# A four-layer graph network on one core: own-feature work of 12 tiles moved to the start of layer 1, and another way to end layer 2

## The chip, the core and the metric

The kernel runs on one core of a Trainium2 chip. The metric is the device time in microseconds of one execution, the median of several runs. TensorE is PE (its weight loads PEld), VectorE is DVE, ScalarE is ACT, GpSimd is POOL, SyncE is SP. DMAs are issued from the queues of SP, ACT and POOL; the indirect ones, that gather rows by an index column, from POOL.

## The reference

A graph of 6250 nodes (49 tiles of 128) and 100,000 edges, sorted by destination (782 tiles of 128 edges). The destinations crowd at low nodes, so that tile 0 alone takes over 14,000 edges.

```python
h = relu(layernorm(x))                                    # 256 features
h = h @ W1_self + mean(h[src] by dst) @ W1_neigh + b1     # layer 1, 512
hp = relu(h @ W2_pool + b2_pool)
h = h @ W2_self + max(hp[src] by dst) @ W2_neigh + b2     # layer 2
h = ((sum(h[src] by dst) + h) / (deg + 1)) @ W3_neigh + b3
h = h @ W4_self + mean(h[src] by dst) @ W4_neigh + b4
out = x + h @ W_fc + b_fc
```

The kernel multiplies weights together beforehand, so that a layer's result is not formed where only its products are needed. Layer 1 writes hp (with Wa = W1_self W2_pool and Wb = W1_neigh W2_pool), layer 2 writes r.

## The kernel before, in words

`fast_path` has a prologue and four layers.

**Layer 1** (`sums`, L442, with `done1`, L1094) makes sums over neighbours in two ways. The edges of node tiles 0 to 7 go through count matrices: `build` makes one-hot tiles (ACT L337 and L338, DVE L340), PE counts with them (L346), and `dense` multiplies the counts with the node rows Z1 that stay on the chip (L564). These pieces are a list that `Hub` steps through, paced by the gathers. The edges from tile 308 on, for node tiles 8 to 48, are gathered: for each of 474 edge tiles POOL gathers 128 rows of `tab_h` into a ring of 14 (L483), DVE makes a one-hot of the destinations (L479), PE multiplies three bf16 parts into `pg` (L505), and after each group of four DVE adds `pg` to the accumulators of the node tiles that the group can hold (L534). A planner (`g_of`) gives each node tile a first and a last group; tile 37's last is 173 of 195, tile 48's is 195. When the last one is in, `done1(d)` is queued: a generator of which one step is taken for each gather, two at a time in flight. It forms the mean m1 (ACT L1103), turns the node's own features h0 (six products of Z1 with a bf16 identity, L1111) and m1 (two f32 transposes, L1114) into one PSUM bank, copies all of it to `th` (ACT L1116), stores `th` in `tab_t` (SP L1117, 256 KB), multiplies the own half with Wa (L1124) and the other half with Wb (L1127) into one bank, adds the bias row `crow` (DVE L1130), applies Relu (ACT L1131) and stores hp in `tab_p` (SP L1132). A list `aside` has work of which one step is taken for each gather too: `tail_checks` (20 steps on DVE) and `segments` (68 steps, with twelve loads on SP).

**Layer 2** walks the edges in another order: six blocks of 52, 100, 220, 180, 130 and 100 steps, the last block first. A step gathers 128 rows of hp (POOL L1475, 256 KB), and DVE keeps a running maximum along each partition's stretch of edges (L1456). Every second row tile is stored in `rows2` (SP L1460). A node's edges can run on from one partition to the next. So at a block's end `carry(b, last)` turns the last row tile (L1316), makes a scan along the partitions (L1324, L1328), gathers the rows where the partitions' first nodes end (POOL L1331, index `fixI`), turns the carry back (L1339), takes the maximum with it (DVE L1342) and stores the result in a part of `rows2` of its own (SP L1343). Then a node tile is begun by `done2(d)`: `totals` gathers its maximum from each block that can hold its edges (POOL L1351; four buffers) and loads `th` back (ACT's queue L1357); `done2` takes the maximum over blocks (DVE L1366), transposes (L1370, ACT L1373), multiplies `th` with usA (L1377) and usB (L1380), the maximum with un (L1383), and splits the result into three bf16 parts (L1391 to L1399), stored as r in `tab_r` (L1400). Tiles are begun last one first, none while a block's carry is under way, at least 11 steps apart and no faster than `NT * (at - FIRST_AT) / (T - 20 - FIRST_AT)`, FIRST_AT being 112. Tiles 6 to 37 are also used at once for layer 3's products (`early_products`, L564 with `ae`; their sums are added at L1241), 1/32 of what is left for each step. By the planner only tile 0 has edges in block 0, the last one that is worked; it also has some in block 1. Tile 1 has edges in blocks 1 and 2, tiles 2 to 9 in block 2 alone. `node_rows` (`finding`) works out the rows that the totals are gathered from, some steps at a time.

**Layers 3 and 4** gather r and its product again with `sums`; layer 3 can gather only when all of `tab_r` is written.

Instructions of one engine run in the order in which the framework lays them out. That order follows the program, but an instruction can stand earlier than where the program has it; `keep_in_program_order` forbids that for one instruction.

Of the kernel before, what the change touches and what calls it, by code (L numbers as in the profile page):

```python
# [9 lines left out]
F32 = mybir.dt.float32  # L10
BF16 = mybir.dt.bfloat16
# [4 lines left out]
ALU = mybir.AluOpType  # L16
# [4 lines left out]
P = 128  # L21
# [11 lines left out]
FIRST_AT = 112  # L33
# [44 lines left out]
def fast_path(  # L78
# [15 lines left out]
    nc = tc.nc  # L94
    N, FI = x.shape
    E = src.shape[0]
    FH = W1_self.shape[1]
# [7 lines left out]
    KI = FI // P  # L105
# [978 lines left out]
    with ExitStack() as on:  # L1084
# [6 lines left out]
        def h0_row(s):  # L1091
            return Z1[:, s, :]

        def done1(d, acc):  # L1094
            r = rmean[:, d : d + 1]
            nc.vector.tensor_copy(deg[:, d : d + 1], acc[:, FI : FI + 1])
            nc.vector.tensor_scalar_max(r, acc[:, FI : FI + 1], 1.0)
            nc.vector.reciprocal(r, r)
            o = only[:, d : d + 1]
            nc.vector.tensor_scalar(o, acc[:, FI + 1 : FI + 2], float(P), None, op0=ALU.mult)  # L1100
            nc.vector.tensor_add(o, o, acc[:, FI + 2 : FI + 3])
            m1 = wk.tile([P, FI], F32, name="m1")
            nc.scalar.activation(m1, acc[:, :FI], AF.Copy, scale=r)  # L1103
            yield 1
            yield 1
            yield 1
            pt = bank(pst, "pt", "pt_m", (2 * KI, P))
            for k in range(KI):
                for part in range(3):
                    c = part * FI + k * P  # L1110
                    nc.tensor.matmul(pt[:, k, :], Z1[:, d, c : c + P], ident_b,  # L1111
                                     start=(part == 0), stop=(part == 2))
            for k in range(KI):
                nc.tensor.transpose(pt[:, KI + k, :], m1[:, k * P : (k + 1) * P], ident)  # L1114
            th = wk.tile([P, 2 * KI, P], F32, name="th")
            nc.scalar.copy(th, pt)  # L1116
# [6 lines left out]
            for k in range(KI):  # L1123
                nc.tensor.matmul(ph, th[:, k, :], Wa[:, k, :], start=(k == 0), stop=False)  # L1124
            yield 1
            for k in range(KI):
                nc.tensor.matmul(ph, th[:, KI + k, :], Wb[:, k, :], start=False,  # L1127
                                 stop=(k == KI - 1))
            hp = wk.tile([P, FH], F32, name="hpf")
            nc.vector.tensor_add(hp, ph, crow)  # L1130
# [10 lines left out]
        for d in range(H1):  # L1141
            work += merged(denses[d], builds[d + 1]) if d + 1 < H1 else denses[d]
        hub = Hub(made.rest() + work)
        sums(wk, psg, tab_h, FI, srcT, keyT, JC * P, H1, done1, 14, hub, counts=3, todo=todo, rest=24,
             aside=[tail_checks(wk), segments()])
    layer1.close()


    def node_rows(pool, psm):
# [28 lines left out]
        for b, tb in reversed(list(enumerate(BLOCKS))):  # L1178
# [26 lines left out]
            nc.vector.tensor_scalar(pF, pF, float(kept[b] * P + 1), None, op0=ALU.add)  # L1205
            nc.vector.tensor_sub(pF, pF, t_)
            nc.vector.tensor_mul(pF, pF, off)
            nc.vector.tensor_add(t_, t_, pF)
# [9 lines left out]
        for k in range(4):  # L1218
# [6 lines left out]
                nc.vector.tensor_tensor(over[:, H1:], lim[:, k, H1:], beg[:1, H1:], op=ALU.is_gt)  # L1225
            nc.vector.tensor_reduce(bad[:1, 4 + k : 5 + k], over, AX.X, ALU.max)


    span3 = ctx.enter_context(tc.tile_pool(name="span3", bufs=1))
    jb = g_of[H3][0] * G  # L1230
# [15 lines left out]
    with tc.tile_pool(name="fl2c", bufs=1) as ck, ExitStack() as late:  # L1246
# [66 lines left out]
        def carry(b, last):  # L1313
# [7 lines left out]
            for k in range(KH):  # L1321
# [9 lines left out]
            nc.gpsimd.indirect_dma_start(  # L1331
                out=fix, out_offset=None, in_=rows2[0 : run_at[b] + n_of[b] - P, :],
                in_offset=bass.IndirectOffsetOnAxis(ap=fixI[:, b : b + 1], axis=0),
# [9 lines left out]
            nc.sync.dma_start(runs[b][n_of[b] - P :, :], fix)  # L1343
            for _ in range(4):
                yield

        def totals(d):
            tots = []
# [118 lines left out]
        for b in reversed(range(NB)):  # L1467
# [57 lines left out]
            next(end)  # L1525
            ends.append(end)
            last_b = b
        for _ in finding:
            pass
        for _ in end:  # L1530
            pass
        tiles += [d for d in reversed(range(NT)) if b_of[d][0] == 0]
        while tiles or now:
            if tiles and len(now) < 2:
                now.append(done2(tiles.pop(0)))
            for g in list(now):
                if next(g, 0) == 0:
                    now.remove(g)
# [776 lines left out]
```

## Time and profile before

| what | us |
|---|---|
| median of 3 runs (2750.1 to 2760.69) | 2751.69 |
| profiled execution, its own time | 2753.24 |
| its span | 2751.4 |
| layer 1's gathers, first to last issue | 104.9 to 712.7 |
| layer 2's first gather of X | 738.26 |
| layer 2's last gather of X is issued | 1833.91 |
| layer 3's first gather | 1873.46 |

Times within the profile count from the start of the span. A row of the timeline gives start, duration, engine, line, operation, the tiles written and read, and in brackets how long the engine had been idle and what ended that. A row by stretch gives for each engine the busy time and the number of instructions in it, then the granted clock of PE as a share of the full one, the share of the DMA engines' time that was used, and GB/s. A row of a group gives the count, the busy time and the mean in ns of one record; a product in f32 with 512 columns leaves two records. A DMA that POOL issues is busy only while it is being issued; the data land later.

### The profile page before, as it was taken

The numbers are of one execution on the slowest core, as the hardware profiler recorded it, in microseconds if no ns is written. First come the engines' busy times: TensorE is split into PE (matmuls) and PEld (weight loads), VectorE is DVE, ScalarE is ACT, GpSimd is POOL, SyncE is SP. The second block draws the span as 40 slices with busy tenths as digits, with TensorE's granted clock in tenths as the row PEclk, the third lists the DMA queues.
The fourth block names the chain that finished last, engine by engine and source line by source line (L and its number), as shares of the span: only waits on it lengthen the run. The fifth ranks groups of instructions, "written<-read, shape, count | busy, mean of one in ns | idle before, by whom it ended". The sixth has DMA issues, their size and how long they took to land.

```text
span 2751.4 us, 39155 instructions
## 1 busy us (share of the span) xinstructions
PE 2372.0 (86%) x11540; PEld 1281.9 (47%) x11671; DVE 2071.6 (75%) x5542; ACT 906.2 (33%) x2177; POOL 1942.6 (71%) x2267
## 2 busy tenths in 40 slices
PE   3578999999887666798899969976999999999998
PEld 2245666776553322343344424432444444565554
DVE  8888777765599898789889988862667776466665
ACT  5467777763278786321311111110000101000000
POOL 6477777776467776777777777744777776677775
PEclk9799999999898787899999989998999999999999
DMA  9566777777699999999999999978999998888886
GB/s 286 154 170 192 208 211 217 229 220 211 207 362 356 328 360 340 364 352 350 327 358 356 359 340 340 343 251 313 373 380 389 387 368 303 259 239 241 240 243 198
DMA packets 350747, 806.43 MB, mean 293 GB/s; under 512 B 56014, under 2 KB 147638, under 8 KB 350492
## 3 DMA queue, kind: packets, MB, share of 16 engines
q0 software_dynamic: 146160, 514.05, 56.8%
q1 hardware_dynamic: 137784, 207.04, 20.7%
q10 hardware_dynamic: 66580, 82.73, 9.0%
q8 instruction: 94, 1.54, 0.2%
q14 instruction: 129, 1.06, 0.1%
HBM read 605.25 MB, written 199.17 MB: 292 GB/s over the span
## 4 chain that ended last, share of the span: by engine, by line
PE 32%; DMA 27%; DVE 8%; issue 5%; POOL 3%; ACT 0%; ACTq 0%; SPq 0%; DVEq 0%; POOLq 0%
DMA X<-rows,srcIf 12%; PE pd L564 11%; PE pg L505 6%; PE pd L556 4%; DMA rows<-X 3%; DVE run L1456 3%; DMA ring<-tab_r,srcE 3%; DMA ring<-tab_s,srcE 3%; DVE X L1456 2%; PE pd L557 2%; POOL X L1475 2%; PE pg L500 2%; PE pm_prf L1383 2%; DMA zt<-tab_r 2%; PE pm_prf L1377 1%
## 5 line engine op out<-in xcount | busy, mean ns | idle before, releaser
L1475 POOL DMA_INDIRECT X<-rows,srcIf x782 | 744.1, 952 | 276.4 <-issue 148.2
L1456 DVE SCALAR_TENSOR_TENSOR run<-run,samef,X 128x512 f32<-128x512 f32 x758 | 571.4, 754 | 45.3 <-DMA X<-rows,srcIf 41.4
L505 PE MATMUL pg<-ring,hot 128*128 128x259 bf16 (+1 forms) x2432 | 516.0, 322 | 68.4 <-DMA ring<-tab_h,srcT 39.5
L483 POOL DMA_INDIRECT ring<-tab_h,srcT x474 | 455.6, 961 | 157.6 <-issue 58.5
L534 DVE SCALAR_TENSOR_TENSOR acc<-pg,M,acc 128x256 f32<-128x256 f32 (+2 forms) x694 | 356.8, 539 | 116.0 <-PE pg L505 83.8
L483 POOL DMA_INDIRECT ring<-tab_r,srcE x342 | 333.7, 976 | 132.0 <-issue 59.4
L564 PE MATMUL pd<-r,ae 128*128 128x512 bf16 x1493 | 367.6, 384 | 37.2 <-DVE acc L1241 35.1
L483 POOL DMA_INDIRECT ring<-tab_s,srcE x314 | 299.8, 955 | 116.5 <-PE pg L501 35.2
L505 PEld LDWEIGHTS <-hot 128*128 128x128 bf16 x2448 | 240.3, 99 | 278.7 <-issue 120.1
L1456 DVE SCALAR_TENSOR_TENSOR X<-X,samef,run 128x512 f32<-128x512 f32 x379 | 281.4, 743 | 48.8 <-issue 17.8
L556 PE MATMUL pd<-zt,ac 128*128 128x512 bf16 x835 | 290.0, 380 | 7.4 <-DMA ac<-tab_a 5.8
L564 PEld LDWEIGHTS <-ae 128*128 128x128 fp8e4 x1536 | 151.2, 99 | 252.0 <-issue 107.0
L557 PE MATMUL pd<-zt,ac 128*128 128x256 bf16 x882 | 241.1, 273 | 2.7 <-DVE zt L312 0.2
L479 DVE TENSOR_SCALAR hot<-iota_bf,keyE 128x128 bf16<-128x128 bf16 x656 | 159.8, 268 | 106.6 <-PE pg L505 76.4
L564 PE MATMUL pd<-zt,ac 128*128 128x512 bf16 x797 | 221.2, 379 | 0.9
L1383 PE MATMUL pm_prf<-unf,hTf 128*128 128x512 f32 x392 | 191.3, 616 | 3.0 <-ACT hTf L1373 3.0
L338 ACT ACTIVATE hs<-ht,onef 128x128 bf16<-128x128 bf16 x396 | 153.8, 393 | 107.5 <-PE pb L346 106.4
L564 PE MATMUL pd<-Z,A 128*128 128x256 bf16 (+1 forms) x1176 | 184.3, 273 | 0.4 <-ACT A L351 0.3
L479 DVE TENSOR_SCALAR hot<-iota_bf,keyT 128x128 bf16<-128x128 bf16 x474 | 126.8, 276 | 53.8 <-PE pg L505 52.2
L346 PE MATMUL pb<-hm,hs 128*128 128x392 bf16 x461 | 147.9, 345 | 13.8 <-DVE hm L340 13.3
L337 ACT ACTIVATE ht<-iota_bf,sk 128x128 bf16<-128x128 bf16 x396 | 153.1, 398 | 8.4
L1391 ACT CAST r<-pm_prf 128x512 bf16<-128x512 f32 x49 | 28.7, 585 | 376.2 <-PE pm_prf L1383 303.3
(347 smaller groups left out, 3597.9 us busy)
## 6 DMA issues: line engine op xcount, KB each, us to landing
rows<-X SPq DMA_DIRECT2D x385, 256.0 KB
tab_r<-r ACTq DMA_DIRECT2D x49, 384.0 KB
tab_t<-th SPq DMA_DIRECT2D x49, 256.0 KB
rows<-hpf SPq DMA_DIRECT2D x49, 256.0 KB
th<-tab_t ACTq DMA_DIRECT2D x49, 256.0 KB
X<-rows,srcIf POOLq DMA_INDIRECT x782, 5.7
ac<-tab_a ACTq DMA_DIRECT2D x90, 112.0 KB
tab_h<-Z SPq DMA_DIRECT2D x16, 579.0 KB
```

Source lines behind the costliest of these rows:

```text
L337: nc.scalar.activation(t, iota_b, AF.Abs, bias=sk[:, r : r + 1])
L338: nc.scalar.activation(hots[0], t, AF.Relu, bias=one, scale=-1.0)
L479: nc.vector.tensor_scalar(hot[j], iota_b, keyT[:, j - jb : j - jb + 1], None, op0=ALU.is_equal)
L483: nc.gpsimd.indirect_dma_start(out=ring[:, j % deep, :], out_offset=None, in_=table, in_offset=bass.IndirectOffsetOnAxis(ap=srcT[:, j - jb ...
L505: nc.tensor.matmul(pg[:, : F + c], hot[j], X[:, part * F : (part + 1) * F + c], start=(k == 0 and part == 2), stop=(k == n - 1 and part == 1),
L534: nc.vector.scalar_tensor_tensor(acc[d], half, m, acc[d], op0=ALU.mult, op1=ALU.add)
L556: nc.tensor.matmul(hold[0], a, z[:, : 2 * F], start=(s == ss[0]), stop=False)
L557: nc.tensor.matmul(hold[0][:, :F], a, z[:, 2 * F :], start=False, stop=(s == ss[-1]))
L564: nc.tensor.matmul(hold[0][:, : F + c], a, z[:, part * F : (part + 1) * F + c], start=(s == ss[0] and part == 2 and s != own), stop=(s == ...
L1383: nc.tensor.matmul(pm, hT[:, c, :], un[:, c, :], start=False, stop=(c == KH - 1))
L1456: nc.vector.scalar_tensor_tensor(put, held, st, row, op0=ALU.mult, op1=ALU.max)
L1475: nc.gpsimd.indirect_dma_start(out=X[:, k, :], out_offset=None, in_=tab_p, in_offset=bass.IndirectOffsetOnAxis(ap=srcI[:, t : t + 1], axis=0),
```

## The change

Three things are changed.

1. `own_ahead` does the own half of `done1` for the last 12 node tiles (37 to 48), as the first entry of `aside`, six steps for each tile: the six products with Z1, the copy to `tho` (256 columns), the store of the first half of `tab_t[d]`, the product with Wa, and the addition of `crow`, kept in a tile `own{d}` for each. For these tiles `done1` then has the other half alone, and adds `own{d}` in the place of `crow`.
2. For block 0, `carry` leaves out the gather of fix, the maximum and the store. It copies the carry that was turned back to `fix` (ACT) and ends. `node_rows` makes for tile 0 a one-hot matrix `takes` that gives each node the partition whose carry it takes. A new `last_done2` takes tile 0 from there: the totals of blocks 1 and 0, a product of `takes` with the carry on PE, kept ahead of the products of `th`, and the maximum over all three.
3. The order of layer 2's late tiles: tiles are paced to `T - 36` instead of `T - 20`; in block 0 they are begun 7 steps apart, also beside a carry; `early_products` are paced to end 16 steps before the end; `last_done2` is begun 14 steps before the end, if no tile is left to begin.

```diff
+        AHEAD = NT - 12
+        own1 = {}
+
+        def own_ahead():
+            for d in range(AHEAD, NT):
+                pt = bank(pst, "pt", "pt_o", (2 * KI, P))
+                for k in range(KI):
+                    for part in range(3):
+                        c = part * FI + k * P
+                        nc.tensor.matmul(pt[:, k, :], Z1[:, d, c : c + P], ident_b,
+                                         start=(part == 0), stop=(part == 2))
+                t = wk.tile([P, KI, P], F32, name="tho", bufs=1)
+                nc.scalar.copy(t, pt[:, :KI, :])
+                nc.sync.dma_start(tab_t[d][:, : KI * P].rearrange("p (k n) -> p k n", n=P), t)
+                yield 1
+                yield 1
+                ph = bank(psm, "pm", "pm_o")
+                for k in range(KI):
+                    nc.tensor.matmul(ph, t[:, k, :], Wa[:, k, :], start=(k == 0),
+                                     stop=(k == KI - 1))
+                    yield 1
+                own1[d] = wk.tile([P, FH], F32, name=f"own{d}", bufs=1)
+                nc.vector.tensor_add(own1[d], ph, crow)
+                yield 1
+                yield 1
...
             th = wk.tile([P, 2 * KI, P], F32, name="th")
-            nc.scalar.copy(th, pt)
-            nc.sync.dma_start(tab_t[d].rearrange("p (k n) -> p k n", n=P), th)
+            nc.scalar.copy(th[:, h0:, :], pt[:, h0:, :])
+            nc.sync.dma_start(tab_t[d][:, h0 * P :].rearrange("p (k n) -> p k n", n=P),
+                              th[:, h0:, :])
...
-            nc.vector.tensor_add(hp, ph, crow)
+            nc.vector.tensor_add(hp, ph, own1[d] if h0 else crow)
...
-             aside=[tail_checks(wk), segments()])
+             aside=[own_ahead(), tail_checks(wk), segments()])
...
+                nc.vector.tensor_mul(off, off, ok)
+                nc.vector.tensor_scalar(pF, pF, 1.0, None, op0=ALU.add)
+                nc.vector.tensor_mul(pF, pF, off)
+                nc.vector.tensor_scalar(pF, pF, -1.0, None, op0=ALU.add)
+                for d in last_tiles:
+                    lanes = bank(psm, "pm", "lanes", (P,))
+                    nc.tensor.transpose(lanes, pF[:, d : d + 1].to_broadcast([P, P]), ident)
+                    yield
+                    takes[d] = pool.tile([P, P], F32, name=f"takes{d}", bufs=1)
+                    nc.vector.tensor_scalar(takes[d], lanes, pidx, None, op0=ALU.is_equal)
...
+            if b == 0:
+                pc = bank(psm, "pm", "pcf")
+                for k in range(KH):
+                    nc.tensor.transpose(pc[:, k * P : (k + 1) * P], cT[:, k, :], ident)
+                nc.scalar.copy(fix, pc)
+                carried.append(fix)
+                return
...
+        def last_done2(d):
+            tots = [total(d, b) for b in range(1, b_of[d][1] + 1)]
+            th = wk.tile([P, 2 * KI, P], F32, name="th2", bufs=4)
+            nc.scalar.dma_start(th, tab_t[d].rearrange("p (k n) -> p k n", n=P))
+            while not carried:
+                yield
+            tots.append(total(d, 0))
+            pc = bank(psm, "pm", "pc_last")
+            nc.tensor.matmul(pc, takes[d], carried[0], start=True, stop=True)
+            pm = bank(psb, "pb", "pm_last")
+            for k in range(2 * KI):
+                us = usA[:, k, :] if k < KI else usB[:, k - KI, :]
+                product = nc.tensor.matmul(pm, th[:, k, :], us, start=(k == 0), stop=False)
+                if k == 0:
+                    tc.keep_in_program_order(product)
+            hm = tots[0]
+            nc.vector.tensor_tensor(hm, hm, pc, op=ALU.max)
+            for t in tots[1:]:
+                nc.vector.tensor_tensor(hm, hm, t, op=ALU.max)
...
-                    early.advance(early.done + math.ceil(early.left() / 32))
+                    early.advance(early.done + math.ceil(
+                        early.left() / max(1, min(32, T - 16 - at))))
+                    if b == 0 and s0 == 0 and k == 0:
+                        for _ in finding:
+                            pass
+                    if b == 0 and not tiles and not ends and last_tiles and at >= T - 14:
+                        now += [last_done2(d) for d in last_tiles]
+                        last_tiles.clear()
...
-                    if (tiles and not ends and at >= begun_at + 11
-                            and begun2 < NT * (at - FIRST_AT) / (T - 20 - FIRST_AT)):
+                    if (tiles and not (b and ends) and at >= begun_at + (11 if b else 7)
+                            and begun2 < NT * (at - FIRST_AT) / (T - 36 - FIRST_AT)):
```

More of the change, by code (lines that the diff above doesn't have):

```diff
@@ L1107, in done1 @@
             pt = bank(pst, "pt", "pt_m", (2 * KI, P))
[L1108 to L1112, printed above, removed]
+            h0 = KI if d >= AHEAD else 0
+            if not h0:
+                for k in range(KI):
+                    for part in range(3):
+                        c = part * FI + k * P
+                        nc.tensor.matmul(pt[:, k, :], Z1[:, d, c : c + P], ident_b,
+                                         start=(part == 0), stop=(part == 2))
             for k in range(KI):
@@ L1122, in done1 @@
             ph = bank(psm, "pm", "pm_hp")
-            for k in range(KI):
-                nc.tensor.matmul(ph, th[:, k, :], Wa[:, k, :], start=(k == 0), stop=False)
+            if not h0:
+                for k in range(KI):
+                    nc.tensor.matmul(ph, th[:, k, :], Wa[:, k, :], start=(k == 0), stop=False)
             yield 1
             for k in range(KI):
-                nc.tensor.matmul(ph, th[:, KI + k, :], Wb[:, k, :], start=False,
+                nc.tensor.matmul(ph, th[:, KI + k, :], Wb[:, k, :], start=bool(h0 and k == 0),
                                  stop=(k == KI - 1))
             hp = wk.tile([P, FH], F32, name="hpf")
-            nc.vector.tensor_add(hp, ph, crow)
+            nc.vector.tensor_add(hp, ph, own1[d] if h0 else crow)
             nc.scalar.activation(hp, hp, AF.Relu)
@@ L1226, in node_rows @@
             nc.vector.tensor_reduce(bad[:1, 4 + k : 5 + k], over, AX.X, ALU.max)
+    takes = {}
+    last_tiles = [d for d in reversed(range(NT)) if b_of[d][0] == 0]
     span3 = ctx.enter_context(tc.tile_pool(name="span3", bufs=1))
@@ L1527, in fast_path @@
             last_b = b
-        for _ in finding:
-            pass
         for _ in end:
             pass
[L1532 to L1535, printed above, removed]
+        now += [last_done2(d) for d in last_tiles]
+        now += [done2(d) for d in tiles]
+        while now:
             for g in list(now):
```

35 lines of the change are left out of this document (31 added, 4 removed).

## The prediction

> **What bounds the kernel now.** I read three views in this order: the busy times by stretch, which tell which engine is full in each stage; the groups of instructions, which give prices; and the timeline at the ends of layers 1 and 2, the two places where the change works.
>
> ```profile
> core 0: us, PE busy (x) PEld busy (x) DVE busy (x) ACT busy (x) POOL busy (x), PEclk, DMA share, GB/s
> 105.00:200.00 95.00, 69.93 (x362) 40.19 (x363) 79.82 (x367) 51.93 (x138) 73.06 (x73) 0.83 0.62 172
> 200.00:300.00 100.00, 86.50 (x570) 58.09 (x569) 74.93 (x343) 71.38 (x207) 75.93 (x80) 0.98 0.69 202
> 300.00:460.00 160.00, 155.11 (x1082) 110.23 (x1082) 120.34 (x449) 119.59 (x325) 121.31 (x128) 1.00 0.71 209
> 460.00:620.00 160.00, 159.98 (x1098) 112.64 (x1097) 116.04 (x429) 108.62 (x289) 121.00 (x129) 1.00 0.75 222
> 620.00:700.00 80.00, 79.91 (x551) 56.42 (x549) 42.30 (x161) 27.24 (x61) 53.86 (x57) 1.00 0.70 208
> 700.00:713.60 13.60, 13.60 (x87) 8.69 (x85) 7.77 (x33) 4.34 (x8) 10.39 (x11) 1.00 0.73 215
> ...
> 1260.00:1620.00 360.00, 341.16 (x1318) 158.76 (x1342) 330.14 (x513) 64.94 (x123) 266.87 (x282) 0.98 0.99 351
> 1620.00:1842.00 222.00, 179.61 (x655) 83.51 (x666) 186.30 (x289) 31.70 (x53) 154.26 (x163) 0.92 0.94 326
> ```
>
> Layer 1's gathers run from 105 to 713.6 us. From 300 to 460 POOL issues 128 in 160 us, one per 1.25 us, and does the same to 620: that is its own pace. From 620 to 700 only 57 come in 80 us, where its pace would give 64, and there PE is full (79.91 of 80). So POOL sets layer 1's pace until 620, and PE after it, with the ring of 14 gathered tiles full. At the start PE has room: 25.1 us idle from 105 to 200 and 13.5 from 200 to 300, together 38.6.
>
> Layer 2 (738 to 1842) has no such room: the DMA share is 0.99 and 0.94 in the two stretches shown, and in the first PE and DVE are over nine tenths busy. At its end everything waits for one chain, shown below.
>
> **Layer 1's own parts.** The prices, first over the kernel, then for the weight product from 105 to 200 us alone:
>
> ```profile
> L1124 PE MATMUL pm_hp<-Wa,th 128*128 128x512 f32 x196 | 94.8, 603 | 0.9 <-ACT th L1116 0.7 <-DVE hpf L1130 0.2
> ...
> L1130 DVE TENSOR_TENSOR hpf<-pm_hp,crow 128x512 f32<-128x512 f32 x49 | 33.9, 691 | 76.1 <-PE pm_hp L1127 63.2 <-ACT A L351 7.2 <-issue 5.6
> ...
> L1116 ACT COPY th<-pt_m 128x512 f32<-128x512 f32 x49 | 28.3, 577 | 42.7 <-PE pt_m L1114 37.1 <-issue 5.6
> ...
> L1111 PE MATMUL pt_m<-ident_b,Z 128*128 128x128 bf16 x294 | 25.3, 219 | 1.9 <-ACT mkf L878 1.9
> ```
>
> ```profile
> L1124 PE MATMUL pm_hp<-Wa,th 128*128 128x512 f32 x8 | 4.9, 696 | 0.0
> ```
>
> An own part is six records of L1111 and four of L1124. Over 49 tiles they are 25.3 and 94.8 us, so 0.52 and 1.93 us for one tile: 2.45 us, and 12 tiles are 29 us of PE. Tile 37's last group is 173 by the planner, so its sums end with gather 388 of 474 (four to a group, and 308 tiles of edges are left to the dense side), near 589 us; all 12 own parts stand behind that point, where PE is full. They go to the first 72 gathers (12 tiles of six steps), 105 to about 198 us. There the product's mean is 696 against 603 ns, so it costs 15% more: about 33 us against 25.1 us idle there and 13.5 in the next 100 us. PE falls some 8 us behind and regains it. The ring stands for 14 gathers, 17.5 us, so POOL should hardly notice; I charge 2 us.
>
> What else is issued early: 12 ACT copies (0.58 us at most) and 12 DVE adds (0.69), and 12 stores on SP of half a tile; the 12 late stores shrink by as much. ACT has 43 us idle there. PE's product now waits for ACT's copy, and behind it on PE stand the sums of the gathers: an exposed wait goes into that same lag. The checks and the segment loads on SP (two for each of six blocks) are moved 72 gathers back and still end by gather 160, before layer 2 needs them.
>
> The end of layer 1 now:
>
> ```profile
> 724.38 0.49 PE L505 MATMUL pg<-ring,hot 128*128 128x259 bf16 x3
> ...
> 725.25 0.48 DVE L534 SCALAR_TENSOR_TENSOR acc<-pg,M,acc 128x259 f32<-128x259 f32 x1
> ...
> 726.55 0.49 ACT L1103 ACTIVATE m<-acc,rmeanf 128x256 f32<-128x256 f32 x1
> ...
> 728.92 0.38 PE L1114 MATMUL pt_m<-identf,m 128*128 128x128 f32 x2
> ...
> 730.02 1.98 PE L1124 MATMUL pm_hp<-Wa,th 128*128 128x512 f32 x4 [0.72 <-ACT th L1116]
> ...
> 731.84 1.88 PE L1127 MATMUL pm_hp<-Wb,th 128*128 128x512 f32 x4
> ...
> 733.82 0.69 DVE L1130 TENSOR_TENSOR hpf<-pm_hp,crow 128x512 f32<-128x512 f32 x1 [3.95 <-PE pm_hp L1127]
> ...
> 737.61 0.24 POOL L1158 IOTA nr<- 128x128 f32 x1 [24.00 <-DMA rows<-hpf]
> ```
>
> POOL's last row shows that the last gather was issued by 713.6 and that it then waited 24 us. With 29 us less behind 589, PE needs less than POOL gives: from 620 to 713.6 it would be about 94 less about 20 (eight or nine tiles), 74 us, where 68 gathers at 1.25 take 85. So POOL's pace decides: the last gather ends at 620 + 85 = 705 instead of 713.6. Then: landing 2.5 us after POOL's instruction (as the fix gather in the next fence: 1846.37 to 1848.85), the last sums 0.5, accumulate and mean 1.8 (725.25 to 727.04), transposes and copy 1.1 (728.92 to 730.02), Wb's product 1.9, and from the add to POOL's release 3.8 (733.82 to 737.61). That is 11.6 us, so 716.6 instead of 737.6: 21 us, less 2 lost early: **19 us**. Bounds: 22, if the early part costs nothing and the halved copy is shorter, and 2, if POOL loses 19 early (worked out under the rivals).
>
> **The end of layer 2.**
>
> ```profile
> 1841.15 0.75 DVE L1456 SCALAR_TENSOR_TENSOR X<-X,samef 128x512 f32<-128x512 f32 x1
> ...
> 1842.64 0.60 PE L1316 MATMUL ptcf<-identf,X 128*128 128x128 f32 x4
> ...
> 1844.80 1.05 PE L1339 MATMUL pcf<-identf,cTf 128*128 128x128 f32 x4
> ...
> 1845.43 0.94 POOL L1331 DMA_INDIRECT fixf<-rows,fixIf  x1 [10.57 <-DMA rows<-X]
> ...
> 1848.85 0.69 DVE L1342 TENSOR_TENSOR fixf<-fixf,pcf 128x512 f32<-128x512 f32 x1 [3.39 <-DMA fixf<-rows,fixIf]
> 1849.57 0.32 SPq L1343 DMA_DIRECT2D rows<-fixf  x1
> 1852.31 0.94 POOL L1351 DMA_INDIRECT tot<-rows,rows_of  x1 [5.93 <-DMA rows<-fixf]
> ...
> 1856.97 0.69 DVE L1366 TENSOR_TENSOR tot<-tot 128x512 f32<-128x512 f32 x1 [7.43 <-DMA tot<-rows,rows_of]
> ...
> 1858.62 3.17 PE L1377 MATMUL pm_prf<-usA,th 128*128 128x512 f32 x4
> 1858.87 0.59 ACT L1373 COPY hTf<-pt_hTf 128x512 f32<-128x512 f32 x1 [11.14 <-PE pt_hTf L1370]
> ...
> 1861.62 1.88 PE L1380 MATMUL pm_prf<-usB,th 128*128 128x512 f32 x4
> ...
> 1863.34 3.60 PE L1383 MATMUL pm_prf<-unf,hTf 128*128 128x512 f32 x8
> ...
> 1866.98 0.59 ACT L1391 CAST r<-pm_prf 128x512 bf16<-128x512 f32 x1 [7.52 <-PE pm_prf L1383]
> ...
> 1869.83 0.33 ACTq L1400 DMA_DIRECT2D tab_r<-r  x1
> ```
>
> The last step ends at 1841.9; tile 0's r leaves at 1869.83: **27.9 us**. In between lie the fix gather, its store and the totals: two gathers and a store in a row, and tile 0's eight f32 records of th that begin only at 1858.62. The new chain, counted from 1841.9: carry transposed back, +4.0 (1844.80 + 1.05); ACT copies it, +4.6; the one-hot product, two f32 records, +5.5; th's eight records behind it, held in order, 3.6 us (as L1383's eight), +9.1. Meanwhile the total of block 0 can be gathered where the fix gather stood (1845.43) and lands where its user started, 1848.85 = +6.9; the max after it ends at +7.7, before PE is free. Then transposes 0.6 and copy 0.7, +10.4; eight records of un 3.6, +14.0; the casts and their corrections 2.85 (1866.98 to 1869.83): +16.9. That saves 11 us. **I take 10**; the one-hot's making falls 50 steps earlier, and its transpose and compare are one instruction each. Bounds: 13, if the transposes come ahead of th's records, and 4, if PE runs its 16 records at the pace of 3.17 for four.
>
> The waits that this adds: PE's one-hot product waits for ACT's copy, and behind it stands only tile 0's work; DVE's max waits for PE, and behind it stands only the flag; POOL's total waits for the last store, and behind it stand layer 3's gathers, which wait for r anyway.
>
> [...]
>
> **The pace of layer 2.** Tiles are begun at one in 12.9 steps instead of 13.3 (634 steps for 49 instead of 650), and in block 0 every 7 steps, also beside a pending carry. No work goes or comes; only order. I count nothing, with 7 us either way: 2.5% more PE work for each step from 1260 to 1620, where PE is 341 of 360 us busy, is 9 us, but 42 us of PE idle from 1620 to 1842 takes most of it back; against it, PE's last tiles come sooner.
>
> **Sum.** 19 + 10 = 29. The profiled execution took 2753.24 us (its span 2751.4 and 1.8 around it), 1.5 above the median of the three runs, 2751.69. 2753.24 - 29 = 2724.2; on the median's footing 2722.7. I say **2724**.
>
> **The rivals.**
> 1. *Cold own parts.* PE's clock is 0.83 in the first stretch. If the 12 parts run at half pace (58 us by the groups), they exceed the 25.1 us idle there by 33; the ring covers 14 (17.5 less the 3.4 from a gather's issue to its landing) and POOL loses 19, which its own pace can't give back. Layer 1 then wins 2: 2741, or 2733 at half the loss. Against it: the 696 ns. Chance 0.12. [...]
> 2. *The pace gives back.* The 9 us of PE work above aren't regained, since DVE and POOL are held behind PE: 2733, up to 2742. Chance 0.14.
> 3. *More is won.* From the view of waits:
>
> ```profile
> DVE tot L1366 <- DMA tot<-rows,rows_of: 33.2, 6, 7.5
> ```
>
> Six of the eight maxes over two totals hold DVE, up to 7.5 us; tile 1's is in block 0. If the new order spreads it, those 7.5 us go too: 2716. Chance 0.12.
> 4. *Slower: totals that wait for PE.* There are four buffers for totals, and PE frees them late:
>
> ```profile
> 1736.05 0.94 POOL L1351 DMA_INDIRECT tot<-rows,rows_of  x1 [0.30 <-issue]
> ```
>
> ```profile
> 1803.72 0.59 ACT L1373 COPY hTf<-pt_hTf 128x512 f32<-128x512 f32 x1 [8.27 <-PE pt_hTf L1370]
> ...
> 1826.76 0.59 ACT L1373 COPY hTf<-pt_hTf 128x512 f32<-128x512 f32 x1
> ```
>
> Tile 2's total is asked for at 1736 and turned at 1826. The change asks for tile 1's and tile 0's totals sooner. If a total's buffer is still held when POOL reaches it, the gathers of X behind it on POOL stop, for up to the 23 us between two turned tiles (1803.7 and 1826.8). Two such stops are 46 us: 2770. It decides from 29 us of stops on. Against it: this total itself waited for nothing (0.30). Chance 0.10.
>
> That the change does not do what it says would show as no own part before 200 us; I see nothing that prevents them, and count it in rival 1.
>
> **Numbers.** The forecast, 2716 to 2732, has 0.52; the rivals 0.12, 0.14, 0.12 and 0.10. From 2708 to 2744 the range holds all of the forecast and of the first two and most of the third, and leaves out about 0.15. Half a per cent, 13.8 us, is what a measurement here tells from no change. Below 2738 lie the forecast, the third, 0.05 of the first and 0.10 of the second: 0.79. Within half a per cent lie what is left of those two and 0.03 of the fourth: 0.14; above, 0.07.
>
> **What would show it.** Layer 1: the Wa product of 12 tiles before 200 us; 64 gathers or so between 620 and 700; POOL's wait after the last gather near 12 us instead of 24; the first X near 718. If POOL falls below 73 gathers before 200, rival 1 is at work. Layer 2: some 1100 us from the first X to the last step, as now; a longer stretch speaks for 2 or 4, and 4 shows as a POOL wait on a PE transpose. End: 17 us from the last step to r's store, with no store of fix for block 0. I am wrong if layer 1 ends by 720 and the kernel is no faster.

## The result and the profile after

The changed kernel takes 2728.93 us, the median of five runs (2721.53 to 2733.48); the kernel before took 2751.52 beside it (2748.9 to 2760.69). The ratio is 0.9905, 95% interval 0.9885 to 0.9926: faster, 22.6 us by the medians. Of the changed kernel the profiled execution took 2726.43 us.

The stages, from the first and last rows of their gathers and steps in the two traces:

| stage, us | before | after | difference |
|---|---|---|---|
| layer 1's last gather is issued | 712.66 | 704.05 | -8.6 |
| from there to the first X | 25.6 | 17.4 | -8.2 |
| first X to the end of the last step | 1103.6 | 1102.1 | -1.5 |
| last step to the store of tile 0's r | 27.9 | 20.2 | -7.7 |
| that store to the end | 881.6 | 880.8 | -0.8 |

By these two traces 26.8 us went: 16.8 by layer 1, 7.7 at the end of layer 2. The experiments will show that the middle row, which looks like nothing, hides a loss that single executions can't show.

Layer 1 by stretch, after (columns as in the rows by stretch of before):

```profile
104.00:200.00 96.00, 83.46 (x465) 48.16 (x465) 80.08 (x357) 54.69 (x151) 73.35 (x74) 0.92 0.64 178
...
460.00:620.00 160.00, 158.58 (x1080) 111.18 (x1079) 113.86 (x423) 107.48 (x286) 121.26 (x128) 1.00 0.74 222
620.00:704.00 84.00, 82.21 (x585) 60.28 (x583) 53.16 (x223) 31.67 (x74) 63.48 (x67) 1.00 0.78 232
...
705.00:721.40 16.40, 9.47 (x31) 4.61 (x29) 4.29 (x15) 3.15 (x6) 0.24 (x1) 0.86 0.31 108
```

POOL issues 74 gathers before 200 us and 128 from 460 to 620, as before: the early work cost it nothing. PE took in about 100 more records there, and its granted clock is 0.92 where the row of before has 0.83. From 620 to 704 PE is nearly full too (82.21 of 84 us), so these rows alone don't tell which engine sets the pace there; `skip12` below does. From 620 on POOL issues 67 in 84 us, one per 1.25, as in its own pace before. Behind its last gather POOL waits 15.8 us instead of 24. The end of layer 1 in the timeline of after:

```profile
704.05 0.95 POOL L483 DMA_INDIRECT ring<-tab_h,srcT  x1 [0.30 <-issue]
...
706.78 0.59 PE L505 MATMUL pg<-ring,hot 128*128 128x259 bf16 x2 [1.41 <-DMA ring<-tab_h,srcT]
...
707.80 2.99 PE L1157 MATMUL pm_hp<-Wb,th 128*128 128x512 f32 x4
...
710.63 0.49 PE L505 MATMUL pg<-ring,hot 128*128 128x259 bf16 x3
...
711.72 1.96 PE L1157 MATMUL pm_hp<-Wb,th 128*128 128x512 f32 x4 [0.60 <-DVE hpf L1160]
...
713.52 0.38 PE L1142 MATMUL pt_m<-identf,m 128*128 128x128 f32 x2
...
717.37 0.63 ACT L1161 ACTIVATE hpf<-hpf 128x512 f32<-128x512 f32 x1 [2.25 <-DVE hpf L1160]
...
720.78 0.24 POOL L1188 IOTA nr<- 128x128 f32 x1 [15.78 <-DMA rows<-hpf]
```

The last sums (`pg`, 710.63) stand on PE behind tile 46's product with Wb, whose four records take 2.99 us, and the last tile's transposes (713.52) behind tile 47's product.

The end of layer 2 in the same timeline; the last step ends at 1823.53:

```profile
1824.60 1.46 PE L564 MATMUL pd<-r,ae 128*128 128x512 bf16 x6
...
1826.11 0.60 PE L1361 MATMUL ptcf<-identf,X 128*128 128x128 f32 x4
...
1827.28 0.94 POOL L1403 DMA_INDIRECT tot<-rows,rows_of  x1 [11.13 <-DMA rows<-X]
...
1829.99 2.07 PE L1418 MATMUL pc_last<-fixf,takes 128*128 128x512 f32 x2 [0.68 <-ACT fixf L1380]
...
1831.86 2.46 PE L1422 MATMUL pm_last<-usA,th 128*128 128x512 f32 x4
...
1832.10 0.69 DVE L1426 TENSOR_TENSOR tot<-tot,pc_last 128x512 f32<-128x512 f32 x1 [3.17 <-PE pc_last L1418]
...
1834.15 1.88 PE L1422 MATMUL pm_last<-usB,th 128*128 128x512 f32 x4
...
1837.14 3.70 PE L1435 MATMUL pm_last<-unf,hTf 128*128 128x512 f32 x8 [0.67 <-ACT hTf L1433]
...
1843.74 0.33 ACTq L1443 DMA_DIRECT2D tab_r<-r  x1
```

The gather and the store of fix are gone, the total of block 0 is asked for while PE turns the carry, and `th`'s product stands where it hides behind the maxima. But the carry's transposes start 2.6 us after the last step (before: 0.7), as PE still holds a product of tile 1 and early products, and from 1829.99 on PE is slow for some us: 2.07 us for two f32 records, then 2.46 for four, where the next four take 1.88.

### The profile page after: what moved, and what is told of

The parts are those of the page before. It is cut to its first block, busy times and chain, and to the rows that moved or that the text cites. A ratio compares the mean times of both kernels' runs of the same rounds, so it can differ in the third digit from the quotient of the medians.

```text
span 2724.6 us, 39212 instructions
## 1 busy us (share of the span) xinstructions
PE 2368.6 (87%) x11542; PEld 1282.5 (47%) x11674; DVE 2076.7 (76%) x5555; ACT 904.5 (33%) x2190; POOL 1938.3 (71%) x2266
## 4 chain that ended last, share of the span: by engine, by line
PE 47%; DMA 28%; DVE 12%; issue 6%; POOL 3%; ACT 1%; ACTq 0%; SPq 0%; DVEq 0%; another core or an unknown queue 0%; POOLq 0%
PE pd L564 12%; PE pg L505 11%; DMA X<-rows,srcIf 11%; DVE run L1555 5%; PE pd L556 4%; DMA rows<-X 4%; DMA ring<-tab_h,srcT 4%; PE pm_hp L1157 3%; DVE X L1555 3%; DMA ring<-tab_s,srcE 2%; PE pd L557 2%; POOL X L1574 2%; PE pm_hp L1154 2%; PE pb L346 2%; PE pg L500 2%
## 5 line engine op out<-in xcount | busy, mean ns | idle before, releaser
L340 DVE TENSOR_SCALAR hm<-iota_w,mk 128x392 bf16<-128x392 f16 x461 | 149.7, 332 | 5.2 <-PE pb L346 4.7
```

## The experiments

Each ratio is to the kernel before, run on the same chip, with its 95% interval. The diffs are to the changed kernel if nothing else is said.

**The three parts alone.** `own_only` and `carry_only` are the kernel before with part 1 or part 2 of the change's diff alone, `pace_only` with part 3 without `last_done2`, which part 2 brings. Part 3 in `pace_only`:

```diff
-                    early.advance(early.done + math.ceil(early.left() / 32))
+                    early.advance(early.done + math.ceil(
+                        early.left() / max(1, min(32, T - 16 - at))))
...
-                    if (tiles and not ends and at >= begun_at + 11
-                            and begun2 < NT * (at - FIRST_AT) / (T - 20 - FIRST_AT)):
+                    if (tiles and not (b and ends) and at >= begun_at + (11 if b else 7)
+                            and begun2 < NT * (at - FIRST_AT) / (T - 36 - FIRST_AT)):
```

> The kernel before with the own parts of tiles 37 to 48 alone moved to the start of layer 1; layer 2 as before. Theory (PE's full stretch behind 589 us is relieved, and POOL's pace sets the rest): the last gather of layer 1 is issued near 704 us instead of 712.7, the first X near 721 instead of 738.3, and the kernel is 16 to 18 us faster, some 2735; layer 2 keeps its 1104 us from the first X to the last step and its 28 us from there to the store of r. Rival (layer 1's gain is made good or lost by what layer 2 then finds): the first X is as early, but layer 2's stretch changes by more than 5 us.

> The kernel before with the one-hot carry and the new last tile alone; layer 1 and the pacing of layer 2 as before. Theory: 738 us at the first X as before; from the last step to the store of tile 0's r some 20 us instead of 28; the kernel is 7 to 9 us faster, 2743 to 2745. Rival (the end is shorter only because the late tiles were paced to be out of PE's way): with the old pacing PE's products of tile 1 and the early ones stand ahead of the carry, and the end is above 24 us; the kernel is less than 4 us faster.

> The kernel before with the new pacing of layer 2's late tiles and early products alone. Theory (only order changes, and DVE's wait for tile 1's totals stays): from the first X to the last step 1104 us, give or take 4, the end as before, 28 us; the kernel within 5 us of before. Rival of the prediction (2.5% more PE work in each step where PE is full, not regained): 5 to 10 us slower. Rival (late tiles out of the way): 3 us or more faster.

| kernel | median, us | ratio | interval | us by the ratio |
|---|---|---|---|---|
| own_only | 2737.81 | 0.9931 | 0.9915 to 0.9947 | -19.0 |
| carry_only | 2745.16 | 0.9962 | 0.9948 to 0.9977 | -10.5 |
| pace_only | 2764.5 | 1.0027 | 1.0013 to 1.0041 | +7.4 |

The kernel before took 2756.96 beside them. Parts 1 and 2 are worth what the prediction gave them, 19 (14.6 to 23.4) and 10 (6.3 to 14.3). Part 3 is no zero: it costs 7.4 us (3.6 to 11.3). The three add to -22, the result.

Their traces: in `own_only` the last gather is issued at 704.15, the first X comes at 719.89, and layer 2 takes 1106.5 and 28.0 us, as its theory has it. In `carry_only` tile 0's r leaves 16.9 us after the last step, sooner than the 20 expected, and tile 1's, the last, after 18.8; its rival falls. In `pace_only` the stretch from the first X to the last step is 1108.9 us, and by the median its theory (within 5 us of before) falls: the rival of the prediction came.

**Half of the own parts** (`own6`):

```diff
-        AHEAD = NT - 12
+        AHEAD = NT - 6
```

> The changed kernel with own parts ahead for the last six tiles instead of twelve. Theory (PE sets the end of layer 1 until POOL's pace does): six parts of 2.45 us take 15 us off PE's full stretch, all of which shows, so the first X comes near 723 to 724, only some 2 us later than with twelve; the kernel within 4 us of the changed one. Rival (each part is worth the same, 16.8 us for twelve): first X near 730, the kernel 8 us slower than the changed one.

Measured: 2743.13 us, 0.9946 (0.9927 to 0.9965). Its row by stretch for 620 to 700:

```profile
620.00:700.00 80.00, 79.91 (x564) 57.45 (x563) 43.98 (x165) 29.06 (x65) 52.65 (x57) 1.00 0.68 200
```

And POOL's last gather and its wait behind it:

```profile
714.54 0.94 POOL L483 DMA_INDIRECT ring<-tab_h,srcT  x1 [0.30 <-issue]
730.24 0.24 POOL L1188 IOTA nr<- 128x128 f32 x1 [14.76 <-DMA rows<-hpf]
```

PE is full and POOL gets 57 gathers out, just as before; the first X is at 730.89. That is 7.4 us earlier than before, where 12 parts brought 16.8: the theory's 723 to 724 falls, the rival's 730 came. But the parts aren't alike. The last gather, at 714.54, is no sooner than without any part ahead (712.66, 714.26 and 716.09 in `before`, `carry_only` and `pace_only`); the whole gain stands behind it, 16.4 us instead of 25.6. For the six tiles are worked late: from 680 to 738 PE has 33 records of the product with Wa in `before`, and 8 here. So the last six parts shorten what PE has left behind the last gather, and the six ahead of them (tiles 37 to 42) bring the last gather itself forward, from 714.54 to 704.05. That the two halves are worth about the same is chance.

**Still less on PE** (`skip12`, which leaves out the product with Wa for tiles 25 to 36), to see whether more than 12 would bring more:

```diff
-            if not h0:
+            if d < AHEAD - 12:
                 for k in range(KI):
                     nc.tensor.matmul(ph, th[:, k, :], Wa[:, k, :], start=(k == 0), stop=False)
```

> The changed kernel without the product of the own features with Wa for tiles 25 to 36 (their hp and what follows lacks that term): 23 us less work on PE behind the middle of layer 1. Theory (with 12 own parts moved, POOL's pace sets layer 1): last gather at 702 to 705 and first X at 718 to 724, as without the edit. Rival (PE, still 22.3 of 24 us busy at the end, sets it): first X earlier by 5 us or more, 716 or less.

Measured: 2739.13 us, 0.9930 (0.9909 to 0.9950), no shorter. Two of its rows by stretch:

```profile
460.00:560.00 100.00, 90.64 (x662) 65.69 (x660) 73.11 (x272) 70.52 (x190) 75.64 (x81) 1.00 0.78 227
...
640.00:680.00 40.00, 37.21 (x279) 28.28 (x278) 18.93 (x74) 7.48 (x15) 30.30 (x32) 1.00 0.77 224
```

PE now has 9.4 us to spare from 460 to 560, and POOL still issues one gather per 1.25 us (32 from 640 to 680): the last gather at 705.02, the first X at 722.88, no sooner than with the product (721.43 and 724.28 in two executions of the changed kernel). So the theory holds: 12 parts reach POOL's floor up to the last gather, and more would be worth nothing there. That the kernel as a whole takes longer than the changed one isn't layer 1's doing: from the first X to the last step its trace has 1112.5 us, the longest of all, for which the edit gives no reason.

**The pace** (`again` is the changed kernel itself; `nopace` has the old order of part 3 altogether, `at20` its pace alone):

```diff
-                            and begun2 < NT * (at - FIRST_AT) / (T - 36 - FIRST_AT)):
+                            and begun2 < NT * (at - FIRST_AT) / (T - 20 - FIRST_AT)):
```

> The changed kernel itself, beside its variants, so that they can be compared on the same chip. Both theories: 0.990 of the kernel before, with first X 720 to 722, 1102 to 1106 us of layer 2 from first X to last step, 20 us from the last step to r's store.

> The changed kernel with parts 1 and 2 alone: the late tiles keep the old order (paced to T - 20, 11 steps apart, none beside a carry; early products at 1/32 of the rest). Theory (the pace gives back what part 3 alone lost, 7.5 us with 3.6 to 11.3): parts 1 and 2 add up, 0.9931 x 0.9962 = 0.9893, so 3 to 8 us faster than the changed kernel, and gathers 400 to 440 of layer 2 take 62 us instead of 68. Rival (the pace is needed once the end is short, since tile 1 is then late): no faster than the changed kernel, and over 20 us from the last step to r's store.

> The changed kernel with tiles paced to T - 20 as before; the rest of part 3 (7 steps apart and beside a carry in block 0, early products to T - 16) stays. Theory: the loss is in the earlier pace, which takes more node tiles into the stretch where PE has no room: as fast as with the old order altogether, 3 to 8 us under the changed kernel. Rival: the loss is in block 0's denser order: equal to the changed kernel within 2 us.

| kernel | median, us | ratio | interval |
|---|---|---|---|
| again | 2736.74 | 0.9925 | 0.9908 to 0.9943 |
| nopace | 2731.67 | 0.9919 | 0.9899 to 0.9938 |
| at20 | 2727.97 | 0.9897 | 0.9878 to 0.9917 |

The kernel before took 2758.16 here. `at20` is 8.8 us under `again` by the medians, `nopace` 5.1, though its ratio can't be told from that of `again`; its end is no longer (19.1 us, tile 1's r being the last; tile 0's leaves after 17.0), so the earlier pace isn't needed for `last_done2`. `again` itself came a little later than expected, with the first X at 724.28. The comparison of the paces was made a second time, on another occasion, with the edit of the next experiment in both kernels (`tail_hold`, which is "the run before" in what follows, against `at20_hold`): 2735.58 against 2729.31, ratios 0.9914 (0.9901 to 0.9928) and 0.9893 (0.9878 to 0.9908), 6.3 us. In each comparison the intervals of the two ratios overlap; that both, and `pace_only`, go the same way is what shows the loss. In the traces of `again` and `at20` 5.3 us of the difference stand at the first X already, which the edit doesn't reach, so 8.8 is likely too much.

> The run before with tiles paced to T - 20. A second comparison of the two paces, on another occasion. Theory (the pace of T - 36 costs): 5 to 9 us under the run before, as 8.8 the first time. Rival (that was scatter of layer 2's stretch from execution to execution): within 3 us of it.

Where it goes: one execution scatters too much (the stretch from first X to last step was 1100.3 to 1106.5 us in seven profiles with T - 20, 1102.1 to 1112.5 in seven with T - 36), but the means, 1103.2 and 1108.4, differ by 5.2, and two short stretches carry it: gathers 240 to 280, behind the second block's end at 230, take 60.9 us on average with T - 20 and 62.9 with T - 36, and gathers 400 to 440, around the third's at 410, take 62.0 and 65.3 (the seven with T - 20 61.4 to 63.8, `nopace` the highest; the seven with T - 36 64.0 to 68.2). The two stretches in the rows of `at20_hold`:

```profile
1053.93:1115.09 61.16, 37.73 (x100) 17.35 (x101) 54.46 (x135) 31.02 (x71) 44.53 (x48) 0.70 0.98 346
1277.42:1338.82 61.40, 49.71 (x201) 23.23 (x200) 50.12 (x91) 24.40 (x49) 44.41 (x48) 0.89 0.98 344
```

And of `tail_hold`:

```profile
1055.27:1118.91 63.64, 41.12 (x117) 18.94 (x117) 53.14 (x130) 36.94 (x86) 45.74 (x48) 0.81 0.98 347
1280.86:1345.16 64.30, 54.40 (x216) 25.11 (x214) 49.94 (x89) 18.65 (x36) 45.50 (x48) 0.95 0.96 336
```

Each row spans 40 gathers of X. With the earlier pace PE does 3.4 and 4.7 us more in them, POOL gathers one total more in each (8 for 7, and 7 for 6), and they take 2.5 and 2.9 us more, at a DMA share of 0.96 to 0.98 in both kernels: another node tile there is paid for in time. Whether its work on PE or its bytes hold the stretch up is not told apart by these runs.

**The end of layer 1** (`tail_hold`): the last four gathers take no step of the node tiles.

```diff
-                for i, t in enumerate(list(pair)):
+                for i, t in enumerate(list(pair) if j < T - hold else ()):
```

> The changed kernel, but the last four gathers of layer 1 take no step of the node tiles, so that the last sums pg stand ahead of tile 46's product with Wb on PE. Theory (that product, 1.9 us or 3.0 at half clock, stands in the way of the last sums): 14 to 15 us from the last gather's issue to the first X instead of 15.7 to 19.0, so 2 to 3 us faster. Rival (what is pushed behind the last sums comes back as a later last tile, in order on PE): 16 to 19 us, no faster.

From its timeline:

```profile
703.16 0.95 POOL L483 DMA_INDIRECT ring<-tab_h,srcT  x1 [0.30 <-issue]
...
708.37 0.80 PE L505 MATMUL pg<-ring,hot 128*128 128x259 bf16 x3 [1.75 <-DMA ring<-tab_h,srcT]
...
708.97 2.89 PE L1157 MATMUL pm_hp<-Wb,th 128*128 128x512 f32 x4
...
721.74 0.24 POOL L1188 IOTA nr<- 128x128 f32 x1 [17.64 <-DMA rows<-hpf]
```

The last sums come sooner, at 708.37, but the first X 19.2 us behind the last gather, no sooner than in the changed kernel (17.4 and 19.0). The rival holds: tile 46's product only moved behind them, and it still runs slowly (2.89 us).

**The end of layer 2** (`th_first`): `th`'s eight records ahead of the carry's way back.

```diff
-            while not carried:
-                yield
-            tots.append(total(d, 0))
-            pc = bank(psm, "pm", "pc_last")
-            nc.tensor.matmul(pc, takes[d], carried[0], start=True, stop=True)
+            while not turned:
+                yield
             pm = bank(psb, "pb", "pm_last")
             ...
+            while not carried:
+                yield
+            tots.append(total(d, 0))
+            pc = bank(psm, "pm", "pc_last")
+            nc.tensor.matmul(pc, takes[d], carried[0], start=True, stop=True)
```

> The changed kernel, but tile 0's eight th records on PE stand between the carry's transposes and its way back, where PE waits for DVE's scan, instead of behind the one-hot product. Theory (they are on the chain of the end): r's store 16 to 17 us after the last step instead of 20.2, so 3.5 us faster than the changed kernel. Rival (they fill a wait for the total of block 0, or push the carry's way back later): 19 to 21 us, no faster.

Measured: 2734.17 us, 0.9923 (0.9905 to 0.9942), and 21.4 us from last step to store: no gain. Its timeline from the one-hot product on:

```profile
1840.01 1.12 PE L1428 MATMUL pc_last<-fixf,takes 128*128 128x512 f32 x2 [0.67 <-ACT fixf L1380]
...
1841.90 0.69 DVE L1432 TENSOR_TENSOR tot<-tot 128x512 f32<-128x512 f32 x1
...
1842.65 1.12 PE L1435 MATMUL pt_hTf<-identf,tot 128*128 128x128 f32 x4 [1.51 <-DVE tot L1432]
...
1844.44 6.11 PE L1439 MATMUL pm_last<-unf,hTf 128*128 128x512 f32 x8 [0.67 <-ACT hTf L1437]
```

The maxima no longer have a product behind which to hide, and un's eight records take 6.11 us instead of 3.70. The same time in rows by stretch:

```profile
1841.00:1842.00 1.00, 0.14 (x1) 0.00 (x0) 0.79 (x2) 0.00 (x0) 0.00 (x0) 1.00 0.00 0
1842.00:1843.00 1.00, 0.35 (x2) 0.36 (x3) 0.59 (x1) 0.00 (x0) 0.00 (x0) 0.75 0.00 0
1843.00:1844.00 1.00, 0.76 (x4) 0.36 (x2) 0.00 (x0) 0.20 (x1) 0.00 (x0) 0.50 0.00 0
...
1846.00:1848.00 2.00, 2.00 (x3) 0.67 (x2) 0.00 (x0) 0.00 (x0) 0.00 (x0) 0.50 0.00 0
...
1850.00:1852.00 2.00, 1.14 (x5) 0.34 (x4) 0.61 (x4) 0.81 (x2) 0.00 (x0) 1.00 0.00 0
```

From 1841 to 1843, while DVE takes the maxima, PE is busy for 0.49 us; its granted clock is 0.50 from about 1842.5 to 1849.3. So, by this one profile, `th`'s product is no burden on that chain: moved ahead of it, it left PE without work and the end no shorter. `at20_hold_split`, which starts from `at20_hold` ("the run before" in its text), follows from that: usA's four records early, usB's four behind the one-hot product.

```diff
+            for k in range(KI):
+                product = nc.tensor.matmul(pm, th[:, k, :], usA[:, k, :], start=(k == 0), stop=False)
             ...
             nc.tensor.matmul(pc, takes[d], carried[0], start=True, stop=True)
+            for k in range(KI):
+                product = nc.tensor.matmul(pm, th[:, KI + k, :], usB[:, k, :], start=False, stop=False)
```

> The run before with tile 0's th records shared out: usA's four between the carry's transposes and its way back, usB's four behind the one-hot product, so that PE has work while DVE takes the maxima. Theory (th_first lost its gain as PE idled there and fell to half clock, 6.1 us for un's eight records instead of 3.7): un's eight records at 3.7, and 16.5 to 17.5 us from the last step to r's store. Rival (the half clock comes from elsewhere): un's eight over 5 us, 19 to 21 us.

Its timeline:

```profile
1834.91 1.13 PE L1428 MATMUL pc_last<-fixf,takes 128*128 128x512 f32 x2 [0.67 <-ACT fixf L1380]
...
1835.87 1.88 PE L1430 MATMUL pm_last<-usB,th 128*128 128x512 f32 x4
...
1837.59 0.61 PE L1440 MATMUL pt_hTf<-identf,tot 128*128 128x128 f32 x4
...
1838.87 3.70 PE L1444 MATMUL pm_last<-unf,hTf 128*128 128x512 f32 x8 [0.67 <-ACT hTf L1442]
...
1845.47 0.33 ACTq L1452 DMA_DIRECT2D tab_r<-r  x1
```

Un's eight are at 3.70 again and the store follows the last step (1828.45) by 17.0 us. The kernel takes 2726.89 us, 0.9877 (0.9861 to 0.9894): the lowest median of those beside it, 31.6 us under the kernel before (2758.51) and 8.7 under `tail_hold`, most of that by the pace. From `at20_hold` (2729.31) its ratio can't be told; in the traces the end is 17.0 for 19.2 us, and `at20`, which has the end of `at20_hold`, took 18.2 for it, so that one us of the difference need not be the edit's.

## Why the prediction was right, and where it was not

Forecast 2724 us, measured 2728.93, within the forecast's own 2716 to 2732.

*Layer 1, 19 us.* Right in its mechanism: alone it is 19.0, in the pair of traces 16.8. POOL lost nothing of the 2 us charged early, PE's room sufficed, and POOL's pace took over from 620 on, with its last gather at 705.0 as worked out (704.05 and its 0.95). That the floor is POOL's, `skip12` shows; PE's work from there on was not the 74 us of the sum but 82.2, so the margin was thin. That the figure agrees to the tenth is chance: its interval is 9 us wide, and the 2 us that weren't lost early stand against 4.2 that were missed at the end. There the 11.6 us behind the last gather are 15.8. The sum went through the last tile alone; in the trace tile 46's product and tile 47's stand on PE between its steps, and PE's granted clock was 0.50 from about 706.6 to 710.0. By the last rows of `pg`, 710.63 + 0.49 instead of 708.0, that is 3.1 us. Of the other 1.1, 0.5 is the wait of the last tile's transposes behind tile 47's product (713.02 to 713.52), and 0.3 the way from the add to POOL's release (4.1 us instead of 3.8).

*End of layer 2, 10 us.* Right: alone 10.5, in the pair 7.7. The chain is the one forecast, in the order forecast, and without part 3 it holds to the tenth: in `carry_only` the transposes start 0.7 us after the last step, un's records end at +14.0 and tile 0's r leaves at +16.9 (tile 1's, the last, at +18.8). In the changed kernel the 16.9 are 20.2. Of the 3.3, 1.8 are the start: in part 3's order PE holds tile 1 and early products for 2.6 us, where the sum had 0.7. The rest is PE at a clock of 0.50, from about 1829.6 to 1833.0: the one-hot product took 2.07 us and usA's four records 2.46, where `at20` has 1.13 and 1.88. The text had a bound for a slow PE but did not count on it (16 records at 3.17 us for four are 5.5 us more by its own figures, which makes the bound 5.5 and not 4). In `at20`, with that order but for the pace, it was 18.2.

*Pace of layer 2, 0 with 7 either way.* This is the step that failed, in size just beyond its own bound: "42 us of PE idle from 1620 to 1842 takes most of it back". It doesn't: part 3 costs 7.4 us alone, and its pace is worth 8.8 and 6.3 when taken out. The loss arises at block borders before 1350, where the DMA share is 0.96 to 0.98 and PE takes 8.1 us more in the two stretches, and it isn't given back later. So rival 2 came, with nearly its own 9 us of PE work not regained (that PE holds the others there is not shown), beside the forecast's gains: 29 us were forecast, 22.6 came, and the 6.4 that are missing are of its size.

*The other rivals.* 1: did not come; the early parts were not slow (592 ns in the middle for a record of their product, where the sum took 696), PE's clock there was not lower but higher (0.92 for 0.83), and POOL kept its pace with 74 gathers before 200 us; eleven of the twelve additions of `crow` were done by then. 3: did not come; tile 1's total still holds DVE, by the view of waits of after:

```profile
DVE tot L1465 <- DMA tot<-rows,rows_of: 7.4, 1, 7.4
```

4: did not come; tile 1's totals and tile 0's of block 1 were asked for from 1785.9 to 1790.9, and POOL stopped for none of them over 0.3 us. Tile 0's total of block 0 (1827.28) waited only for the last store of X.

The sum of the 10 us has PE at the full pace through that chain. That was the author's estimate: no run shows that a chain of short waits always keeps it. In the changed kernel the clock fell at about 706.6, in a wait of 1.41 us, and at about 1829.6, in a chain of waits of at most 0.68:

```profile
705.00:706.00 1.00, 0.36 (x3) 0.08 (x1) 0.49 (x1) 0.00 (x0) 0.00 (x0) 1.00 0.67 241
706.00:707.00 1.00, 0.22 (x2) 0.19 (x3) 0.00 (x0) 0.00 (x0) 0.00 (x0) 0.81 1.20 369
707.00:708.00 1.00, 1.00 (x6) 0.94 (x5) 0.00 (x0) 0.13 (x1) 0.00 (x0) 0.50 0.30 102
...
709.00:710.00 1.00, 1.00 (x2) 0.34 (x1) 0.00 (x0) 0.00 (x0) 0.00 (x0) 0.50 0.39 131
710.00:711.00 1.00, 1.00 (x5) 0.29 (x3) 0.11 (x1) 0.00 (x0) 0.00 (x0) 0.99 0.00 0
...
1828.00:1829.00 1.00, 0.47 (x4) 0.21 (x3) 0.93 (x5) 0.00 (x0) 0.22 (x1) 1.00 0.20 20
1829.00:1830.00 1.00, 0.33 (x3) 0.13 (x2) 0.00 (x0) 0.58 (x1) 0.00 (x0) 0.80 0.70 224
1830.00:1831.00 1.00, 1.00 (x1) 0.49 (x2) 0.00 (x0) 0.00 (x0) 0.00 (x0) 0.50 0.91 362
...
1832.00:1833.00 1.00, 1.00 (x3) 0.48 (x2) 0.87 (x2) 0.00 (x0) 0.00 (x0) 0.50 0.00 0
1833.00:1834.00 1.00, 1.00 (x3) 0.42 (x3) 0.51 (x1) 0.00 (x0) 0.00 (x0) 0.99 0.00 0
```

In `at20` it stayed at 1.00 at the end of layer 1, with a wait of 1.83 us:

```profile
705.87 0.38 PE L505 MATMUL pg<-ring,hot 128*128 128x259 bf16 x2 [1.83 <-DMA ring<-tab_h,srcT]
```

```profile
704.00:705.00 1.00, 0.04 (x1) 0.00 (x0) 0.49 (x1) 0.00 (x0) 0.00 (x0) 1.00 0.82 256
705.00:706.00 1.00, 0.13 (x2) 0.15 (x3) 0.00 (x0) 0.00 (x0) 0.00 (x0) 1.00 0.76 213
706.00:707.00 1.00, 1.00 (x7) 0.75 (x6) 0.00 (x0) 0.37 (x1) 0.00 (x0) 1.00 0.07 26
```

So the length of the wait alone doesn't tell these cases apart; what does is not shown here.

## What to carry to other kernels

Work that one engine does late can pay in full beside an early stage where that engine has room, up to the point where the next engine's pace is the floor (here 12 parts, 19.0 us alone, and in `skip12` no earlier last gather with less on PE); count records until that point and no further. Reordering that adds no work isn't free where the stretch is full already (here 7.4 us alone): look at the stretches behind each border, not at the mean, and test the order alone. On a short serial chain at the end of a stage, independent products that fill PE's waits can be worth more in their place than out of the way, as the end of 21.4 us with all eight records moved and of 17.0 with four shows.

## What the runs showed of the hardware that was not expected

- PE's granted clock fell to 0.50 in a chain with no wait over 0.68 us (`after`, about 1829.6 to 1833.0), and stayed at 1.00 with a wait of 1.83 us (`at20`, 704 to 706). Where it was 0.50, four f32 records took 2.99 us instead of 1.88 at the end of layer 1, and un's eight 6.11 instead of 3.70. The time of a sparse end of a stage differs from execution to execution: of the ten traces with twelve own parts ahead, `own_only` and `at20` took 15.7 and 16.2 us from the last gather to the first X, with a clock of 1.00 from 704 to 714 and from 702 to 709; the other eight took 17.4 to 19.2, two executions of the changed kernel 17.4 and 19.0, and two of the eight, `after` and `skip12`, had 0.83 from 704 to 714.
- From 104 to 200 us PE's granted clock was 0.83, 0.86 and 0.90 in the three traces without own parts there (64 to 70 us of PE busy), 0.95 in `own6` with six (74.6), and 0.90 to 0.98 in the ten with twelve (81 to 85). One pair of traces, such as 0.83 and 0.92, says less, as the clock scatters by 0.07 in itself.
- Layer 2's stretch of 782 gathers scatters by 6 us between kernels that have the same pace there (1100.3 to 1106.5 in seven profiles), so that a change of 5 us in it can't be read from one pair of traces.
